# The last norm of a decoder layer: its first mean over five blocks of rows, not six

## The chip, the cores and the metric

The kernel runs on one core of a Trainium2 chip. The metric is the time of one execution on the device in microseconds (us), less is better. Before the change the median of three runs is 2515.79 us (2514.77 to 2517.98). All engines named are those of that core: TensorE (PE in the profile, with PEld for its weight loads), VectorE (DVE), ScalarE (ACT), GpSimd (POOL) and SyncE (SP), whose queue issues nearly all DMAs.

## What is computed

One decoder layer on eight sequences of 100 tokens, 1024 features each, in float32: a retention layer, a cross-attention over 722 context rows and the own tokens, and a gated feed-forward layer. After each of the three the input is added and the sum is normalised over the features. The change lies in the last of the three norms:

```python
def _layernorm(x, axis=-1, eps=1e-05):
    m = jnp.mean(x, axis=axis, keepdims=True)
    v = jnp.var(x, axis=axis, keepdims=True)
    return (x - m) / jnp.sqrt(v + eps)
...
    gate = jnp.einsum('bsd,hd->bsh', x, w_gate)
    up = jnp.einsum('bsd,hd->bsh', x, w_up)
    gated = jax.nn.silu(gate) * up
    return jnp.einsum('bsh,dh->bsd', gated, w_down)
...
x = _layernorm(x + _L0_ffn_ref(x, L0_ffn_w_gate, L0_ffn_w_up, L0_ffn_w_down), axis=-1)
```

## The kernel before

**Layout.** Activations lie with their features on the 128 partitions and the tokens along the free dimension. The 1024 features are KT = 8 blocks of rows, 0 to 7, and the 800 tokens two halves of N = 400. So y, the sum that is to be normalised, is eight tiles of 128 x 400 for each half, and a mean over the features is a sum over the eight blocks and over the partitions. The second is made on TensorE: a matmul whose weights are a 128 x 128 matrix with the same number everywhere (onem holds 1/1024; onem7 holds 1/896) leaves the column sum in all partitions of a PSUM tile.

**Products.** For float32 accuracy every operand is split into a high and a low part, and each product is three matmuls (L86 to L88 in mm3). The function proj makes one block of rows for one half: 8 x 3 = 24 matmuls of 128 x 400 into one PSUM bank. PSUM has banks of three tags: a (3), s (4) and v (1); acc_tag takes a and s in turn for successive calls.

**The last stage** (L976 to L1003). The hidden features of the feed-forward layer are worked through in four quarters. The first three use a scheme with seven products in place of eight; the last quarter is done here, block by block: proj multiplies block m of the last quarter's weights by z3[half], and L994 adds it to y[:, m], which holds the input and the other three quarters already. The first half of the tokens goes first; it splits the weights and keeps all eight, and the second half uses them again. There add_up (L254) also sums the blocks into s1.

**The norm of the first half** (norm_root, then scaled): when all eight blocks are there, the mean by one matmul (L279), eight subtractions (L281), eight squares on ScalarE (L260) summed on VectorE (L265), the variance by one matmul (L283), its inverse root by Ln and Exp on ScalarE and a correction step on VectorE (inv_root, L113 to L120), and eight multiplications (L271), each followed by the DMA of its block to the output. This runs while TensorE makes the products of the second half.

**The norm of the second half** would stand at the end with nothing behind it, so it is begun before all blocks are there. norm_early takes the mean of the blocks so far by one matmul (L294) and subtracts it from them (L297). The blocks that come later have the same number subtracted when their product is added (L993, L994). Then norm_more adds each of them to two sums that stay open in PSUM: delta (L305), which gives the distance of the true mean from the one that was used, and var (L299 for the early blocks' squares together, L306 for those of each later one). norm_late then takes the square of delta on ScalarE (L312), subtracts delta from all blocks (L316), takes the square of delta from var (L313), makes the inverse root, and calls scaled. In exact arithmetic the result is the same whichever blocks come early; the number of early blocks is the argument first, and the factor f = 7 / first turns onem7's 1/896 into the mean over first blocks:

```python
f = (KT - 1) / first
for m in range(first):
    nc.vector.scalar_tensor_tensor(y[:, m], mean, -f, y[:, m], ALU.mult, ALU.add)
```

norm_early, norm_more and norm_late also serve out_proj, where seven blocks come early (the default of first).

**What sets the order.** Each engine runs its own list of instructions strictly in order and waits on counters of the others. The lists are made when the program is built: a scheduler simulates a time line and takes, for each engine, the ready instruction of the highest priority, so an instruction can stand at another place of its list than in the text. Thus in the second half's last products the one of block 7 (its weights lie in the tile f, its bank has the tag a) stands ahead of the one of block 6 (weights z, tag s). Once built the order is fixed: if an instruction isn't ready in fact, everything behind it on its engine waits.

In the built program the end looks like this. TensorE: products of blocks 4, 5 and 7, L294, product of block 6, two L305, L299, two L306. VectorE: additions for blocks 4 and 5 with the eight multiplications of the first half (L271) between them, six L297, two L993, one L265, L994 for block 7, L994 for block 6, four L265, eight L316, L313, two steps of the root, eight L271. ScalarE: eight squares, with L312 between the sixth and the seventh, and the three steps of the root. A float32 matmul with unsplit operands (L279, L283, L294, L299, L305, L306) is shown as two matmul records.

Of the kernel before, what the change touches and what calls it, by code (L numbers as in the profile page):

```python
# [20 lines left out]
KT = D // P  # L21
# [18 lines left out]
def decoder_layer(ctx, tc, xT, cT, w1, wo1, w2, wo2, wc, w3, wd, gw, qw, kw, trig, dec, mask, out):  # L40
    nc = tc.nc

    def sbuf(name, bufs, side=None):
        return tc.tile_pool(name=name, bufs=bufs, side=side, reuse_waits="tile")
# [51 lines left out]
    def acc_tag():  # L96
        turn[0] += 1
        return "as"[turn[0] % 2]

    def proj(w, z, n=N, tag="a"):  # L100
        acc = bank(tag)[:, :n]
        for k in range(KT):
            t = z[k // QT]
            mmw(acc, w, k, t[:, 0, k % QT, :n], t[:, 1, k % QT, :n], k == 0, k == KT - 1)
        return acc
# [146 lines left out]
    def add_up(s1, y, m):  # L252
        if m > 0:
            nc.vector.tensor_tensor(s1, y[:, 0] if m == 1 else s1, y[:, m], ALU.add)  # L254
# [14 lines left out]
    def scaled(y, r, dst, z=None):  # L269
        for m in range(KT):  # L270
            nc.vector.scalar_tensor_tensor(y[:, m], y[:, m], -0.5, r, ALU.mult, ALU.mult)  # L271
            if z is not None:
                split(z[m // QT][:, :, m % QT], y[:, m])
            nc.sync.dma_start(out=dst(m), in_=y[:, m])

    def norm_root(y, s1, p):
        n = y.shape[2]
        mean = bank("s")[:, :n]
        nc.tensor.matmul(mean, onem, s1, start=True, stop=True)  # L279
        for m in range(KT):  # L280
            nc.vector.tensor_tensor(y[:, m], y[:, m], mean, ALU.subtract)  # L281
        var = bank("v")[:, :n]
        nc.tensor.matmul(var, onem, squares(y, p, range(KT)), start=True, stop=True)  # L283
        vs = p.tile([P, n], F32, tag="vs", name="vs")
        nc.scalar.copy(vs, var)
        return inv_root(p, vs, eps_ln, n)
# [4 lines left out]
    def norm_early(y, s1, p, first=KT - 1):  # L291
        n = y.shape[2]
        mean = bank("s")[:, :n]
        nc.tensor.matmul(mean, onem7, s1, start=True, stop=True)  # L294
# [3 lines that stand above are left out]
        var, delta = bank("v")[:, :n], bank("s")[:, :n]  # L298
        nc.tensor.matmul(var, onem, squares(y, p, range(first)), start=True, stop=False, skip_group_check=True)  # L299
        return mean, var, f, delta, first  # L300

    def norm_more(y, early, p, m):

        _, var, _, delta, first = early
        nc.tensor.matmul(delta, onem, y[:, m], start=m == first, stop=m == KT - 1, skip_group_check=True)  # L305
        nc.tensor.matmul(var, onem, squares(y, p, [m]), start=False, stop=m == KT - 1, skip_group_check=True)  # L306

    def norm_late(y, early, p, dst, z=None):
        _, var, _, delta, _ = early
        n = y.shape[2]  # L310
        vs = p.tile([P, n], F32, tag="vs", name="vs")
        nc.scalar.activation(vs, delta, AF.Square)  # L312
        nc.vector.tensor_tensor(vs, var, vs, ALU.subtract)  # L313
        r = inv_root(p, vs, eps_ln, n)
        for m in range(KT):
            nc.vector.tensor_tensor(y[:, m], y[:, m], delta, ALU.subtract)  # L316
        scaled(y, r, dst, z)
# [9 lines left out]
    def load_raw(src):  # L327
        st = wp.tile([P, KT * P], F32, tag="wst", name="wst", bufs=3)
        if isinstance(src, list):
            for i, s in enumerate(src):  # L330
                nc.sync.dma_start(out=st[:, i * H:(i + 1) * H].rearrange("p (u c) -> p u c", u=QT), in_=s)
        else:
            nc.sync.dma_start(out=st, in_=src)
        return st

    def w_split(src, w=None):
        if w is None:
            w = wp.tile([P, 2, KT * P], FR, tag="w", name="w", bufs=4)
        split(w, src)
        return w  # L340
# [573 lines left out]
    def next_slot():  # L914
        slots.append(slots.pop(0))
        return slots[-1]()
# [23 lines left out]
    def down_w(q, m):  # L940


        w = wd[q * QT:(q + 1) * QT, m // QT].rearrange("u p c -> p u c")
        c = m % QT * 2 * P
        return [w[:, :, c + i * P:c + (i + 1) * P] for i in range(2)]
# [31 lines left out]
    with sbuf("ln3", 2, "right") as lnp:  # L977
        ws = []
        for half in range(2):
            y = rows(half)  # L980
            s1 = lnp.tile([P, N], F32, tag="s1", name="s1", bufs=2)
            early = None
            for m in range(KT):
                if half == 0:
                    w = None
                    if m >= QT:
                        w = next_slot().rearrange("p l k n -> p l (k n)")[:, :, :KT * P]
                    ws.append(w_split(load_raw(down_w(QT - 1, m)), w))
                elif m == KT - 2:
                    early = norm_early(y, s1, lnp, m)  # L990
                acc = proj(ws[m], z3[half], tag=acc_tag())
                if early:
                    nc.vector.scalar_tensor_tensor(y[:, m], early[0], -early[2], y[:, m], ALU.mult, ALU.add)  # L993
                nc.vector.tensor_tensor(y[:, m], y[:, m], acc, ALU.add)  # L994
                if early:
                    norm_more(y, early, lnp, m)
                else:
                    add_up(s1, y, m)
            dst = lambda m, half=half: out[:, m, half * N:(half + 1) * N]
            if half == 0:  # L1000
                scaled(y, norm_root(y, s1, lnp), dst)
            else:
                norm_late(y, early, lnp, dst)  # L1003
# [71 lines left out]
```

## Time and profile before

| | |
|---|---|
| median of three runs | 2515.79 us (2514.77 to 2517.98) |
| the profiled execution's own time | 2517.7 us |
| its span, first to last instruction | 2515.9 us |
| TensorE busy in the span | 2465.4 us (98%) |
| VectorE, ScalarE, GpSimd busy | 1992.2, 1343.5, 481.2 us |
| mean granted TensorE clock | 0.993 |
| TensorE busy from 2480 to 2500 us | 18.89 of 20.00 |
| TensorE busy from 2500 us to the end | 2.30 of 16.00 |
| VectorE busy in the same two stretches | 13.91 and 10.28 |

The profile is of one execution; its time is 1.8 us more than its span, and 1.9 us more than the median of the runs. The page also draws the span in 40 slices of 63 us, busy tenths in each; the last of them holds the end of the last stage:

```profile
PE   8999999999899999999999999999999999999997
PEld 8999999999899999999999999999999999998997
DVE  7678876568989798899999999866987777666656
ACT  6667676335767565556566566533544544432221
```

TensorE is at nine tenths or more almost everywhere, so an engine beside it costs time only where TensorE waits for it, and at the very end, after TensorE's last product. That end, some 15 us, is where the changed lines stand. In the rows of the timeline the first number is the start in us from the span's beginning, the second the duration; a row that stands for several instructions (x6) has their duration together, and what stands in brackets is how long the engine was idle before the row and which instruction ended the wait.

### The profile page before, as it was taken

What the parts mean: (1) busy time and instruction counts of PE and PEld (TensorE: products, weight loads), DVE (VectorE), ACT (ScalarE), POOL (GpSimd) and SP (SyncE); (2) the same over time, 40 slices, a digit from 0 to 9 for tenths busy, and PEclk for the clock granted to TensorE, in tenths of its full rate; (3) what the DMA queues carried; (4) which work ended last, traced back from release to release, by engine and by line L of the source; (5) the groups of instructions that cost most, each with busy time, mean ns of one, the idle gap of its engine ahead of it and who ended that gap; (6) DMA issues with size and microseconds to landing.
All of it is one profiled execution on the core that took longest, in us unless ns stands there. A gap on an engine that the chain in (4) does not pass through costs nothing.

```text
span 2515.9 us, 37158 instructions
## 1 busy us (share of the span) xinstructions
PE 2465.4 (98%) x14036; PEld 2442.0 (97%) x14036; DVE 1992.2 (79%) x3110; ACT 1343.5 (53%) x2264; POOL 481.2 (19%) x234
## 2 busy tenths in 40 slices
PE   8999999999899999999999999999999999999997
PEld 8999999999899999999999999999999999998997
DVE  7678876568989798899999999866987777666656
ACT  6667676335767565556566566533544544432221
POOL 0111111002645334433433433100000000000000
PEclk9999999999999999999999999999999999999999
DMA  7334445774444654554554554574455445388731
GB/s 240 110 110 127 136 144 187 239 266 148 144 152 133 207 175 142 178 166 151 169 176 144 166 192 135 189 273 152 145 181 192 159 160 167 127 302 311 250 102 53
DMA packets 224450, 433.96 MB, mean 172 GB/s; under 512 B 47338, under 2 KB 168042, under 8 KB 211854
## 3 DMA queue, kind: packets, MB, share of 16 engines
q1 hardware_dynamic: 223118, 427.39, 50.7%
q0 software_dynamic: 1152, 4.19, 1.1%
q8 instruction: 110, 1.80, 0.3%
q14 instruction: 70, 0.57, 0.1%
HBM read 322.18 MB, written 109.35 MB: 172 GB/s over the span
## 4 chain that ended last, share of the span: by engine, by line
PE 89%; DVE 6%; ACT 1%; DMA 1%; issue 1%; SPq 0%; DVEq 0%; ACTq 0%
PE a L88 18%; PE a L86 18%; PE a L87 18%; PE s L88 9%; PE s L87 9%; PE s L86 9%; PE v L88 2%; PE v L86 2%; PE v L87 2%; PE s L491 1%; PE s L688 1%; DVE r L120 1%; DVE r L119 1%; PE s L148 1%; DMA tp<-in_xT 1%
## 5 line engine op out<-in xcount | busy, mean ns | idle before, releaser
L86 PE MATMUL a<-big,w 128*128 128x400 f32 (+2 forms) x1808 | 611.4, 339 | 11.7 <-ACT big L67 7.4
L87 PE MATMUL a<-big,w 128*128 128x400 f32 (+2 forms) x1808 | 611.1, 338 | 0.0
L88 PE MATMUL a<-big,w 128*128 128x400 f32 (+2 forms) x1808 | 609.7, 338 | 0.0
L67 ACT CAST w<-wst 128x1024 fp32r<-128x1024 f32 (+1 forms) x231 | 239.2, 1038 | 389.4 <-PE s L88 130.7
L68 DVE TENSOR_TENSOR w<-wst,w 128x1024 fp32r<-128x1024 f32 (+1 forms) x231 | 281.0, 1218 | 117.0 <-ACT w L67 115.1
L86 PEld LDWEIGHTS a<-big,w 128*128 128x128 f32 x1808 | 341.3, 189 | 13.3 <-ACT big L67 7.7
L87 PEld LDWEIGHTS a<-big,w 128*128 128x128 f32 x1808 | 342.0, 189 | 1.3 <-DVE big L68 0.3
L88 PEld LDWEIGHTS a<-big,w 128*128 128x128 f32 x1808 | 342.0, 189 | 0.9 <-DVE w L68 0.2
L86 PE MATMUL s<-big,w 128*128 128x400 f32 x664 | 230.6, 347 | 0.1
L87 PE MATMUL s<-big,w 128*128 128x400 f32 x664 | 229.2, 345 | 0.0
L88 PE MATMUL s<-big,w 128*128 128x400 f32 x664 | 229.1, 346 | 0.0
L125 POOL PARTITION_ALL_REDUCE ss<-sq x56 | 161.1, 2881 | 336.3 <-DMA zd<-y 167.0
L605 POOL PARTITION_ALL_REDUCE kss<-ksq x64 | 173.2, 2706 | 116.4 <-ACT ksq L604 115.7
L86 PE MATMUL a<-z,w 128*128 128x400 f32 x488 | 168.6, 346 | 8.0 <-ACT r L118 4.3
L88 PE MATMUL a<-z,w 128*128 128x400 f32 x488 | 169.4, 348 | 0.7 <-DVE w L68 0.7
L87 PE MATMUL a<-z,w 128*128 128x400 f32 x488 | 169.4, 347 | 0.0
L87 PE MATMUL s<-z,w 128*128 128x400 f32 x400 | 139.1, 348 | 2.4 <-DVE z L68 2.4
L86 PE MATMUL s<-z,w 128*128 128x400 f32 x400 | 139.9, 350 | 0.0
L88 PE MATMUL s<-z,w 128*128 128x400 f32 x400 | 139.4, 348 | 0.0
L722 ACT ACTIVATE s<-s,rk 128x400 f32<-128x400 f32 x160 | 87.7, 591 | 91.9 <-DVE sm L742 65.5
L86 PEld LDWEIGHTS s<-big,w 128*128 128x128 f32 x664 | 124.6, 188 | 1.4 <-ACT w L67 0.4
L87 PEld LDWEIGHTS s<-big,w 128*128 128x128 f32 x664 | 124.6, 188 | 1.1
(330 smaller groups left out, 5650.9 us busy)
## 6 DMA issues: line engine op xcount, KB each, us to landing
wst<-in_w SPq DMA_DIRECT2D x135, 512.0 KB
w<-wcd SPq DMA_DIRECT2D x64, 1024.0 KB
wst<-in_wo SPq DMA_DIRECT2D x64, 512.0 KB
hd<-h SPq DMA_DIRECT2D x12, 1400.0 KB
wst<-in_wd SPq DMA_DIRECT2D x64, 256.0 KB
big<-o1d SPq DMA_DIRECT2D x16, 800.0 KB
qd<-d SPq DMA_DIRECT2D x32, 400.0 KB
q<-qd SPq DMA_DIRECT2D x32, 400.0 KB
```

Source lines behind the costliest of these rows:

```text
L67: nc.scalar.copy(hi, src)
L68: nc.vector.tensor_tensor(lo, src, f32(hi), ALU.subtract)
L86: nc.tensor.matmul(acc, lh, rh, start=start, stop=False, skip_group_check=chain)
L87: nc.tensor.matmul(acc, lh, rl, start=False, stop=False, skip_group_check=chain)
L88: nc.tensor.matmul(acc, ll, rh, start=False, stop=stop, skip_group_check=chain)
L119: nc.vector.scalar_tensor_tensor(q, ss, eps, q, ALU.add, ALU.mult)
L120: nc.vector.scalar_tensor_tensor(q, q, 3.0, r, ALU.subtract, ALU.mult)
L125: nc.gpsimd.partition_all_reduce(y, x, P, op)
L148: nc.tensor.transpose(tr[0:T, b * P:(b + 1) * P], vt[:, b * T:(b + 1) * T], ident)
L491: nc.tensor.matmul(bt(o)[:, b], vv[:, b * P:(b + 1) * P], pf[:, b], start=True, stop=True)
L605: nc.gpsimd.partition_all_reduce(ss[:, at], sq[:, at], P, RED.add)
L722: nc.scalar.activation(sc, sp, AF.Copy, scale=rk[:, c:c + 1])
```

## The change

In the second half of the tokens, norm_early is called ahead of block 5 rather than block 6. It gets first = m, so five blocks (0 to 4) are summed, taken relative to their mean and squared early; blocks 5, 6 and 7 (before: 6 and 7) go through L993 and norm_more.

```diff
@@ -986,7 +986,7 @@
                     if m >= QT:
                         w = next_slot().rearrange("p l k n -> p l (k n)")[:, :, :KT * P]
                     ws.append(w_split(load_raw(down_w(QT - 1, m)), w))
-                elif m == KT - 2:
+                elif m == KT - 3:
                     early = norm_early(y, s1, lnp, m)
                 acc = proj(ws[m], z3[half], tag=acc_tag())
                 if early:
```

In the order of the built program this moves instructions on three engines. TensorE: L294 stands seven matmuls behind the start of block 7's product; where it stood, between the products of blocks 7 and 6, stands L305 for block 5; after the product of block 6 come L299, L306 for block 5, two L305 (blocks 6 and 7) and two L306. VectorE: behind the eight L271 of the first half come five L297, three L993, one L265, L994 for blocks 5 and 7, three L265, L994 for block 6, and then L316 as before. ScalarE: L312 stands behind all eight squares. The lists of GpSimd and SyncE are the same.

## The prediction

> **What bounds the kernel now.** The page's chain of waits says that TensorE bounds the whole, so I looked for the stretch in which another engine takes over, then read the timeline of that stretch.
>
> ```profile
> PE 89%; DVE 6%; ACT 1%; DMA 1%; issue 1%; SPq 0%; DVEq 0%; ACTq 0%
> ```
>
> Timeline (start, duration in us, engine, line, out<-in, idle before and its releaser), end of the program:
>
> ```profile
> 2484.52 0.57 DVE L254 TENSOR_TENSOR s<-s,y 128x400 f32<-128x400 f32 x1
> ...
> 2488.89 0.57 DVE L994 TENSOR_TENSOR y<-y,a 128x400 f32<-128x400 f32 x1
> 2488.99 0.35 PE L87 MATMUL a<-big,f 128*128 128x400 f32 x1
> ...
> 2491.91 0.34 PE L88 MATMUL a<-big,f 128*128 128x400 f32 x1
> 2492.09 0.83 PE L294 MATMUL s<-s,onem 128*128 128x400 f32 x2
> ...
> 2492.94 0.34 PE L87 MATMUL s<-big,z 128*128 128x400 f32 x1
> 2492.96 2.98 DVE L297 SCALAR_TENSOR_TENSOR y<-s,y 128x400 f32<-128x400 f32 x6 [2.90 <-PE s L294]
> ...
> 2495.86 1.04 DVE L993 SCALAR_TENSOR_TENSOR y<-s,y 128x400 f32<-128x400 f32 x2
> 2496.82 0.56 DVE L265 TENSOR_TENSOR s<-sq 128x400 f32<-128x400 f32 x1
> 2496.95 0.34 PE L88 MATMUL s<-big,z 128*128 128x400 f32 x1
> 2497.31 0.56 DVE L994 TENSOR_TENSOR y<-y,a 128x400 f32<-128x400 f32 x1
> 2497.79 0.56 DVE L994 TENSOR_TENSOR y<-y,s 128x400 f32<-128x400 f32 x1
> 2498.40 1.61 PE L305 MATMUL s<-y,onem 128*128 128x400 f32 x4 [1.10 <-DVE y L994]
> 2500.05 0.50 ACT L312 ACTIVATE vs<-s 128x400 f32<-128x400 f32 x1
> 2500.79 3.93 DVE L316 TENSOR_TENSOR y<-y,s 128x400 f32<-128x400 f32 x8
> ```
>
> TensorE feeds everything until the mean (L294), which stands between the product of block 7 (weights f, issued first) and that of block 6 (weights z). From 2492.96 on VectorE is almost never idle: its list behind the mean, not block 6's product, sets the end. The new mean could use VectorE's gap before 2492.96.
>
> **The change, part by part.** I read the order and the wait counts of both built programs; they differ only here. VectorE loses one L254 and one L265 and does five L297 and three L993 for six and two. ScalarE squares eight blocks either way. TensorE gets one L305 and one L306 more. No DMA is added or moved; SyncE's and GpSimd's queues are as they were.
>
> *The mean earlier.* L294 now stands behind seven matmuls of block 7's product, at 2488.99. It needs the sum over blocks 0 to 4, ready at 2484.52 + 0.57 = 2485.09, so it doesn't wait. VectorE starts L297 0.87 later (2492.09 to 2492.96 now): 2489.86. It has then finished the eight multiplies of the first half, whose next instruction starts at 2488.89 now.
>
> *VectorE until block 5 is complete.* Eight subtractions of the mean at 0.483 (2.90 / 6), 3.86, to 2493.72; one L265, 0.49 (2496.82 to 2497.31): block 5's L994 starts at 2494.21. This addition is now behind the subtractions; before, it ran at 2488.89, ahead of them.
>
> *The wait that the change adds.* L305 for block 5 stands on TensorE between the products of blocks 7 and 6, and waits for exactly that L994. A matmul starts 0.61 after such an addition starts (2497.79 to 2498.40): 2494.82. TensorE has issued the last of block 7 at 2491.91 + 0.67 (one such small product costs 2492.94 - 2492.09 less a normal step of 0.18) = 2492.58; with 0.34 that ends at 2492.92. So TensorE stands idle for 1.90 us. Queued behind L305 are block 6's 24 matmuls, and behind those the addition of block 6 and all that follows. L305 takes the place that L294 had, so block 6 starts 2494.82 - 2492.09 = 2.73 later; its last matmul at 2499.68, its L994 0.39 later (a row pair at 2483.16 and 2483.55) at 2500.07, so its L305 may start at 2500.68.
>
> *The tail.* TensorE first issues L299 and block 5's L306, ready long before, at 0.67 each from 2499.86 to 2501.20; then L305 for blocks 6 and 7 at 2501.20 and 2501.87. The step from the last L305 to L316 is shown bare in the other late norm:
>
> ```profile
> 1740.99 0.83 PE L305 MATMUL s<-y,onem 128*128 128x400 f32 x2
> ...
> 1741.86 0.50 ACT L312 ACTIVATE vs<-s 128x400 f32<-128x400 f32 x1 [2.77 <-PE s L305]
> 1742.39 3.94 DVE L316 TENSOR_TENSOR y<-y,s 128x400 f32<-128x400 f32 x8 [0.90 <-ACT vs L312]
> ```
>
> That is 0.87 + 0.53, so L316 starts at 2503.27 for 2500.79: **+2.5 us**. All behind it is unchanged: the last two L306 end at 2504.1, before L313 at 2507.1 asks for the variance. The two VectorE instructions saved (2 x 0.48) are worth nothing, as VectorE now waits for TensorE; if that wait is gone they come back.
>
> *What an idle TensorE does to its clock.* The trace shows no such stall at this place, so I bound it by all others. Windows (length, PE busy, ..., PEclk third from the end):
>
> ```profile
> 847.42:850.84 3.42, 1.52 (x11) 1.23 (x10) 1.31 (x5) 2.34 (x6) 0.00 (x0) 1.00 0.95 244
> 850.84:854.25 3.41, 3.41 (x14) 3.41 (x13) 1.98 (x8) 0.97 (x5) 0.00 (x0) 0.50 0.97 341
> ...
> 509.50:512.91 3.41, 2.04 (x11) 1.59 (x10) 1.90 (x3) 1.04 (x1) 0.00 (x0) 1.00 1.02 424
> 512.91:516.32 3.41, 3.41 (x20) 3.27 (x19) 3.41 (x8) 1.02 (x2) 0.00 (x0) 1.00 1.01 415
> ```
>
> The granted clock falls to a half at 608.49, 635.80, 676.76, 714.30, 850.84 and 2318.57, all whole multiples of 3.413 apart: it is decided on a fixed grid. I computed TensorE's busy time in every cell of it. Start-up aside, a full-clock cell with 1.52 busy or less is followed by one at half clock; one with 2.04 or more never is; none lies between. At half clock matmuls start 0.333 apart (2322.24 to 2322.57), not 0.182, so a cell loses 3.41 x (1 - 0.182 / 0.333) = 1.55 us, and all of it would fall into block 6's product. The cost is thus 0 or 1.55. A stall of 1.90 leaves 1.51 busy in a cell that holds all of it. With the limit at 1.52, 1.51 of 3.41 positions of the grid do that, 44%; with the limit at 2.04 (1.37 idle suffices, so 0.53 more on each side), 75%; halfway 60%. I take 1.55, by that majority.
>
> The Trainium skill says otherwise: "TensorE: Matmul & The Clock Gate", in its part on the HAM clock gate and that on HAM oscillation, lets the clock fall only after a whole idle window of about 3.4 us. By it this stall would cost nothing more and the sum would be +2.5; the row above, with 1.90 us idle and the next cell at 0.50, contradicts it.
>
> **Sum.** 2.5 + 1.55 = +4.0. The profiled execution has a span of 2515.9 and a time of 2517.7, 1.8 around it; it would become 2519.9 and 2521.7. It was 1.9 above the median of the runs; on that median, 2515.79 + 4.0 = 2519.8. That is 0.16%; a measurement of this kernel can tell about 0.2% (5.0 us) from no change, so I forecast a small loss that counts as no change.
>
> **Rivals.**
>
> *The stall without the clock.* As above, with the grid lying so that no cell sees too little work: 2515.79 + 2.5 = 2518.3. For it: 40% of positions by the halfway limit. Against it: the other 60%.
>
> *Clearly slower: two half-clock cells in a row.* At 2318.57 the first slow cell had 2.52 busy, and the next was slow too; at 676.75 one with 3.17 busy was not. So if a grid edge falls inside the stall, with at least 1.37 idle before it and at least 0.24 behind it, the clock stays low twice: 2.5 + 3.1 = 5.6, 2521.4, +0.22%. It decides from an edge between 2494.29 and 2494.58, 0.29 of 3.41 positions at the most, and with the strict limits (1.90 and 0.89) never.
>
> *Not slower: TensorE doesn't wait.* If block 5's addition is in time, block 6 starts only one small product (0.67) later; its last matmul at 2497.62, then L299, L306 and two L305 at 0.67, L316 at 2501.21: +0.4, 2516.2. For that VectorE would have to be 2 us quicker between the mean and L994 than its rows say. If moreover only VectorE's load counted, the two instructions saved would give -1.0, 2514.8. Against both: the rows of the nine instructions in front.
>
> That the change doesn't act is out: both orders show the mean moved.
>
> **How the numbers follow.** Stall and one slow cell 0.45; stall alone 0.38; two slow cells 0.05; no stall 0.12. Predicted: 2519.8. The range goes from 2516.2, the upper end of the no-stall case, to 2521.4, the two-cell case; within it lie all cases but part of the last and the scatter of the runs (2514.77 to 2517.98). Likeliest case alone: 2518.8 to 2520.8. Slower by over 0.2%: the two-cell case, and a fifth of the forecast, which lies 1.0 below the bound, with scatter: 0.05 + 0.09 = 0.14. Faster by over 0.2% would need -5.0, more than any term here; 0.01 for scatter. Within: 0.85.
>
> **What would show it.** Right: the mean near 2489, L297 five times from about 2489.9, an idle time of about 1.9 before L305 released by L994, block 6's product starting 2.7 later, VectorE idle before L994 of block 6 and before L316. The clock: 0.50 in one cell of 3.41 within block 6's product, and matmuls 0.333 apart. Wrong: L305 for block 5 without idle time; L316 starting before 2502; a difference before 2484, where both programs are equal; or a stall well above 1.9, which would make the slow cell certain.

## The result and the profile after

| | before | changed |
|---|---|---|
| median (lowest to highest) of 22 runs each | 2516.70 us (2514.77 to 2525.07) | 2520.84 us (2518.46 to 2527.34) |
| ratio, 95% interval | | 1.0015 [1.0008, 1.0022] |
| span of the profiled execution | 2515.9 | 2520.4 |
| from the first matmul of block 5's product to L316 | 17.44 | 21.59 |

The medians differ by 4.1 us, 0.16%; the forecast was +4.0. The interval of the ratio is 2.0 to 5.5 us, so the whole times leave room for the rival of +2.5 as well; it takes the traces to decide. In the text below, the distance from the first matmul of block 5's product to the first L316 is called the tail. It leaves out what varies from execution to execution ahead of the last stage, so it compares single traces to some hundredths of a us, where a few whole runs leave 2 us open. Its two ends before are the first matmul below and L316 at 2500.79; VectorE's row below stands directly ahead of that L316.

```profile
2483.35 0.34 PE L86 MATMUL a<-big 128*128 128x400 f32 x1
...
2498.27 2.60 DVE L265 TENSOR_TENSOR s<-s,sq 128x400 f32<-128x400 f32 x4
```

The timeline of the changed kernel, VectorE's rows first (columns as before):

```profile
2490.17 2.50 DVE L297 SCALAR_TENSOR_TENSOR y<-s,y 128x400 f32<-128x400 f32 x5 [0.88 <-PE s L294]
2492.59 1.53 DVE L993 SCALAR_TENSOR_TENSOR y<-s,y 128x400 f32<-128x400 f32 x3
2494.03 0.57 DVE L265 TENSOR_TENSOR s<-sq 128x400 f32<-128x400 f32 x1
2494.51 1.05 DVE L994 TENSOR_TENSOR y<-y,a 128x400 f32<-128x400 f32 x2
...
2502.03 0.57 DVE L994 TENSOR_TENSOR y<-y,s 128x400 f32<-128x400 f32 x1 [4.62 <-PE s L88]
2505.25 3.94 DVE L316 TENSOR_TENSOR y<-y,s 128x400 f32<-128x400 f32 x8 [2.65 <-ACT vs L312]
```

TensorE, from the start of the tail:

```profile
2483.66 0.34 PE L86 MATMUL a<-big 128*128 128x400 f32 x1
...
2489.30 0.83 PE L294 MATMUL s<-s,onem 128*128 128x400 f32 x2
...
2495.13 0.94 PE L305 MATMUL s<-y,onem 128*128 128x400 f32 x2 [1.90 <-DVE y L994]
...
2496.09 0.35 PE L87 MATMUL s<-big,z 128*128 128x400 f32 x1
...
2496.67 0.54 PE L87 MATMUL s<-big,z 128*128 128x400 f32 x1
2497.01 0.54 PE L88 MATMUL s<-big,z 128*128 128x400 f32 x1
...
2501.65 0.34 PE L88 MATMUL s<-big,z 128*128 128x400 f32 x1
2501.83 0.83 PE L299 MATMUL v<-s,onem 128*128 128x400 f32 x2
2502.50 0.83 PE L306 MATMUL v<-sq,onem 128*128 128x400 f32 x2
2503.18 1.51 PE L305 MATMUL s<-y,onem 128*128 128x400 f32 x4
```

The reader is to see two things. Before, VectorE waited 2.90 us for the mean and then ran without a gap; now it waits 0.88, but 4.62 for block 6's product and 2.65 for L312. The engine that sets the end has changed: the wait has gone from VectorE to TensorE, which stands idle for 1.90 us ahead of L305, released by block 5's addition. And from 2496.67 on the matmuls of block 6's product start 0.33 apart rather than 0.18. The windows of the cells around it (a cell is one step of the grid of 3.413 us on which the clock is set) show the granted clock at that place (PE busy first, then the other engines, the granted clock third from the end):

```profile
2493.15:2496.57 3.42, 1.52 (x7) 1.15 (x7) 3.32 (x8) 1.45 (x3) 0.00 (x0) 1.00 0.01 2
2496.57:2499.98 3.41, 3.41 (x12) 3.38 (x11) 0.73 (x2) 0.58 (x2) 0.00 (x0) 0.50 0.00 0
2499.98:2503.39 3.41, 3.41 (x16) 2.80 (x16) 0.57 (x1) 0.55 (x2) 0.00 (x0) 1.00 0.00 0
```

One cell with 1.52 us of work, then exactly one cell at half clock.

### The profile page after: what moved, and what is told of

The parts are those of the page before. It is cut to its first block, busy times and chain, and to the rows that moved or that the text cites. A ratio compares the mean times of both kernels' runs of the same rounds, so it can differ in the third digit from the quotient of the medians.

```text
span 2520.4 us, 37163 instructions
## 1 busy us (share of the span) xinstructions
PE 2469.7 (98%) x14040; PEld 2445.2 (97%) x14040; DVE 1993.9 (79%) x3108; ACT 1343.4 (53%) x2264; POOL 478.7 (19%) x234
## 4 chain that ended last, share of the span: by engine, by line
PE 89%; DVE 6%; DMA 2%; issue 1%; ACT 1%; SPq 0%; DVEq 0%; ACTq 0%
PE a L88 18%; PE a L86 18%; PE a L87 17%; PE s L88 10%; PE s L87 10%; PE s L86 9%; PE v L88 2%; PE v L86 2%; PE v L87 2%; PE s L491 1%; PE s L688 1%; DVE r L120 1%; DVE r L119 1%; PE s L148 1%; DVE d L68 1%
```

## The experiments

The theory: the loss is the wait of TensorE for block 5's addition, with 1.90 us of idle time ahead of L305 and L316 2.5 us later, and the half-clock cell that this idle time brings about, 1.55 us. The main rival: it is the added work, two small matmuls more and a longer row of statistics. Kernels are compared by the tail, where not said otherwise; the ratios are those to the kernel before on the same chip.

### The same work, block 5 first on VectorE (e3_first5)

The edit moves no instruction on TensorE; VectorE takes block 5's L993 and addition as soon as the mean is there, ahead of the five L297. (In this kernel the two steps of block 5 are shown as an L297 and L990.)

```diff
-        for m in range(first):
-            nc.vector.scalar_tensor_tensor(y[:, m], mean, -f, y[:, m], ALU.mult, ALU.add)
+        for m in ([first] if block else []) + list(range(first)):
+            i = nc.vector.scalar_tensor_tensor(y[:, m], mean, -f, y[:, m], ALU.mult, ALU.add); block and (block(y, m) if m == first else m == 0 and tc.keep_in_program_order(i))
...
-                    early = norm_early(y, s1, lnp, m)
+                    early = norm_early(y, s1, lnp, m, lambda y, m: nc.vector.tensor_tensor(y[:, m], y[:, m], proj(ws[m], z3[1], tag=acc_tag()), ALU.add))
...
```

> The same instructions as the changed kernel on every engine, TensorE in the same order; only VectorE takes the two steps of block 5 (L993, its addition) ahead of the five subtractions of the mean. Theory (stall): L305 of block 5 finds its input ready, no idle time before it, no half-clock cell, block 6's product 0.67 us later than before the change, L316 0.4 us later: +0.4 us, ratio 1.0002. Rival (work): nothing is removed, so +4 us as before, ratio 1.0015.

Measured: ratio 0.9999 [0.999, 1.0008]; tail 17.88, +0.44. The timeline, VectorE and TensorE:

```profile
2488.51 0.57 DVE L297 SCALAR_TENSOR_TENSOR y<-s,y 128x400 f32<-128x400 f32 x1 [0.88 <-PE s L294]
2489.12 0.57 DVE L990 TENSOR_TENSOR y<-y,a 128x400 f32<-128x400 f32 x1
2489.61 2.49 DVE L297 SCALAR_TENSOR_TENSOR y<-s,y 128x400 f32<-128x400 f32 x5
...
2499.88 3.94 DVE L316 TENSOR_TENSOR y<-y,s 128x400 f32<-128x400 f32 x8 [2.65 <-ACT vs L312]
```

```profile
2491.23 0.34 PE L88 MATMUL a<-big,f 128*128 128x400 f32 x1
2491.41 0.83 PE L305 MATMUL s<-y,onem 128*128 128x400 f32 x2
2491.78 0.65 PE L86 MATMUL s<-big,z 128*128 128x400 f32 x1
```

Block 5 is complete at 2489.69, well ahead of 2491.41, and L305's row has no idle time. The work is all still there and 3.7 of the 4.15 us are gone. The rival that blames the work for the whole loss falls; 0.44 us are left, which this kernel doesn't take apart.

### The idle time filled (e2_fill)

Two small matmuls are added ahead of L305 of block 5. They write to delta's bank, which L305 then overwrites; block 6's product is held behind L305 (d5 is that L305).

```diff
...
     def norm_more(y, early, p, m):
-
+        for i in range(2 * (early[4] == m == 5)): nc.tensor.matmul(early[3], onem, y[:, 4], start=True, stop=False, skip_group_check=True)
...
-                acc = proj(ws[m], z3[half], tag=acc_tag())
+                with tc.issue_after(d5.ins) if early and m == 6 else nullcontext(): acc = proj(ws[m], z3[half], tag=acc_tag())
```

> The changed kernel with two more small matmuls, whose result is overwritten, between block 7's product and L305 of block 5. Theory (stall and clock apart): L305 still starts when block 5's addition is done, at the same time; the idle time before it falls from 1.90 to about 0.57 us, no grid cell is under 2.8 us of work there, so the clock stays at 1.00 through block 6's product: +2.5 us over the kernel before in every execution, ratio 1.0010, although TensorE does 1.33 us more. If the clock had no part in it: +4 as in the changed kernel. Rival (work): 1.33 more than the changed kernel, +5.4 us, ratio 1.0021.

Measured: ratio 1.0014 [1.0005, 1.0023]; tail 20.06, +2.62. The idle time in the timeline, and the cells' windows:

```profile
2489.54 1.50 PE L303 MATMUL s<-y,onem 128*128 128x400 f32 x4
...
2491.60 0.94 PE L305 MATMUL s<-y,onem 128*128 128x400 f32 x2 [0.56 <-DVE y L994]
```

```profile
2488.17:2491.59 3.42, 2.88 (x13) 1.94 (x11) 3.42 (x9) 0.59 (x3) 0.00 (x0) 1.00 0.00 0
2491.59:2495.00 3.41, 3.40 (x17) 3.10 (x18) 2.08 (x4) 1.55 (x4) 0.00 (x0) 1.00 0.01 2
```

TensorE does two small matmuls more than in the changed kernel, some 1.3 us (the idle time falls from 1.90 to 0.56), L305 starts as late as there (11.47 us behind the first matmul of block 5's product), and the tail is 1.53 us shorter. That is the price of the half-clock cell, with the wait itself left in. The whole runs can't tell the two kernels apart; the trace does.

### The changed kernel again, and four single executions (a2_same, a3_look to a6_look)

> The changed kernel once more, beside the others on the same chip. Theory (stall): TensorE stands idle for 1.9 us before L305 of block 5, released by L994, in this execution too; block 6's product starts 2.7 us later than before the change. Whether the half-clock cell follows depends on where the grid lies: time over the kernel before +2.5 us without it, +4.0 with it, so a ratio between 1.0010 and 1.0016. Rival (work): the loss is the two more small matmuls and the longer statistics at the end; then the same +4, but with no part of it before block 6's product.

Measured: ratio 1.0014 [1.0005, 1.0023]; idle time 1.90, a half-clock cell, tail 21.59. So far every trace of the changed kernel had the slow cell, and the grid's part was not shown. Four more executions were traced for that; all four have the same expectation.

> The changed kernel once more, for its trace alone. Theory: the idle time before L305 of block 5 is 1.90 us each time, but the grid of 3.41 us lies at another place in each execution. If a grid cell holds at least 1.8 us of the idle time, the next one runs at half clock and L316 starts 21.6 us after the first matmul of block 5's product; if a grid edge cuts the idle time so that neither cell holds as much, the clock stays at 1.00 and the distance is 20.0 to 20.1. About half of the looks should be of each kind. Rival (any idle time of this length costs the clock, wherever the grid lies): 21.6 in all looks.

Measured: the idle time is 1.90 in all four; the tails are 21.59, 20.04, 21.63 and 20.04. Windows of the cells in the first (a3_look) and in the second (a4_look):

```profile
2488.64:2492.05 3.41, 1.51 (x7) 1.07 (x7) 3.31 (x8) 1.38 (x3) 0.00 (x0) 1.00 0.01 2
2492.05:2495.46 3.41, 3.41 (x12) 3.39 (x11) 0.81 (x2) 0.67 (x2) 0.00 (x0) 0.50 0.00 0
```

```profile
2488.53:2491.95 3.42, 1.76 (x10) 1.42 (x8) 3.42 (x8) 0.59 (x2) 0.00 (x0) 1.00 0.00 0
2491.95:2495.36 3.41, 3.17 (x16) 2.88 (x17) 2.30 (x5) 1.77 (x4) 0.00 (x0) 1.00 0.01 2
```

The same stall, cut by a grid edge in the second (its L305 starts at 2492.19, the edge is at 2491.95): 1.76 us of work in the cell, and no slow cell; in a6_look 1.82, and none. The rival that any stall of this length costs the clock falls. Six traces of the changed kernel: four with, two without. The whole times of the four (2517.76, 2517.70, 2521.26, 2516.95) don't show it: block 5's product starts at 2479.22, 2480.72, 2482.69 and 2479.97, so they differ by more than the price of a cell before the last stage begins. Start-up aside, five, five, six and five half-clock cells lie ahead of it, so their number alone doesn't explain the differences; the rest stays open.

### L305 of block 5 behind the products (e1_late)

```diff
+        d = nc.tensor.matmul(delta, onem, y[:, m], start=m == first, stop=m == KT - 1, skip_group_check=True); m == 5 and tc.keep_in_program_order(d)
...
+                for k in (range(5, m + 1) if early and m == 6 else [m] if early and m == 7 else []):
+                    norm_more(y, early, lnp, k)
```

> L305 of block 5 is pinned behind block 6's product; the scheduler then also puts most of block 7's product behind that of block 6, and two L305 (blocks 5 and 6) directly behind both. Theory (stall): no idle time between the products, both end as before the change; behind them two L305, L299, L306, L305 of block 7 at 0.67 each, L316 0.4 us later than before the change: +0.4 us, ratio 1.0002. Rival (work): as the changed kernel, +4 us, ratio 1.0015.

Measured: ratio 1.0002 [0.9993, 1.0011]; tail 17.87, +0.43; no idle time between the products. A second way of removing the wait gives the same as the first. VectorE again waits for L312:

```profile
2500.05 3.94 DVE L316 TENSOR_TENSOR y<-y,s 128x400 f32<-128x400 f32 x8 [3.32 <-ACT vs L312]
```

### The variance last (e4_delta_first), and one matmul less (e8_sum)

If the wait is all that spoils the change, the early mean should be of use once it is gone. Both kernels keep e1_late's order; the first puts all matmuls of the variance behind the last L305, the second also adds blocks 5 and 6 on VectorE before one L305 reads the sum (early[5] is the sum of the early blocks' squares).

```diff
+        for k in (range(first - 1, KT) if m == KT - 1 and len(early) > 5 else [] if len(early) > 5 else [m]): tc.keep_in_program_order(nc.tensor.matmul(var, onem, early[5] if k < first else squares(y, p, [k]), start=k < first, stop=k == KT - 1, skip_group_check=True))
...
+        if m == 6: t = p.tile([P, N], F32, tag="d56", name="d56", bufs=1); nc.vector.tensor_tensor(t, y[:, 5], y[:, 6], ALU.add)
+        if m != 5: tc.keep_in_program_order(nc.tensor.matmul(delta, onem, t if m == 6 else y[:, m], start=m == max(first, 6), stop=m == KT - 1, skip_group_check=True))
```

> As the kernel with block 5's L305 behind the products, and the four matmuls of the variance (L299 and three L306 before, now all on L306's line) behind the last L305. Theory (stall): with no idle TensorE between the products, what is left in front of L316 is the addition of block 7, the last L305 and L312. Three L305 stand directly behind the products at 0.67 each, the third reads block 7: L316 starts 0.9 us earlier than before the change, the variance is ready 1 us before L313 asks for it. -0.9 us, ratio 0.9996, beyond what the rounds can tell, so the trace decides: from the first matmul of block 5's product to L316 16.5 us, where the kernel before has 17.4 and the changed one 21.6. Rival (work): not below the kernel before.

Measured: ratio 1.0 [0.9991, 1.0009], by which it is told apart from neither kernel; tail 16.53, -0.91. VectorE:

```profile
2494.14 0.57 DVE L994 TENSOR_TENSOR y<-y,a 128x400 f32<-128x400 f32 x1 [0.23 <-PE a L88]
2496.70 3.94 DVE L316 TENSOR_TENSOR y<-y,s 128x400 f32<-128x400 f32 x8 [1.98 <-ACT vs L312]
```

> As the kernel with the variance behind, and blocks 5 and 6 added to each other on VectorE before one L305 reads them, so two L305 in place of three. Theory (stall): VectorE is idle while block 7's product runs, so the addition costs nothing; the last L305 starts as soon as block 7 is added, 0.5 us earlier: L316 1.4 us earlier than before the change, 16.0 us from the first matmul of block 5's product; ratio 0.9994. Rival (work): not below the kernel before.

Measured: ratio 0.9995 [0.9986, 1.0004]; tail 16.11, -1.33. TensorE behind the last matmul of the products:

```profile
2496.56 0.34 PE L88 MATMUL a<-big,f 128*128 128x400 f32 x1
2496.74 0.83 PE L305 MATMUL s<-d,onem 128*128 128x400 f32 x2
2497.57 0.94 PE L305 MATMUL s<-y,onem 128*128 128x400 f32 x2
2498.34 0.83 PE L306 MATMUL v<-s,onem 128*128 128x400 f32 x2
```

The first L305 fills the time in which block 7 is added, and only one more stands ahead of L312. By the whole runs, this kernel is faster than the changed one (the intervals of the two ratios don't meet) and not told apart from the kernel before; by the trace its tail is 1.33 us shorter than that of the kernel before.

### Four and seven early blocks (e5_four, e6_seven)

The edit is the number alone: KT - 4 or KT - 1 in place of KT - 3.

> Four early blocks, not five. The scheduler takes block 5's product ahead of block 4's, the mean ahead of block 4's, the first half's eight multiplies between the subtractions of the mean. Theory (stall): VectorE completes block 4 at nearly the time when TensorE reaches its L305, which then stands between the products of blocks 7 and 6: an idle time of 0.3 us, no half-clock cell. Two L305 more inside, L299 and two L306 in front of the last two L305: L316 2.2 us later than before the change, ratio 1.0009. Rival (fewer early blocks cost more by themselves): over the changed kernel's +4.

Measured: ratio 1.0015 [1.0006, 1.0024]. Block 5's product comes first here, so the distance is taken from the product behind that of block 3: 22.48 before (2478.31 to 2500.79), 24.87 here, +2.39. The idle time ahead of the first L305 is 0.33 and the clock stays:

```profile
2493.94 0.94 PE L305 MATMUL s<-y,onem 128*128 128x400 f32 x2 [0.33 <-DVE y L994]
```

The ratio holds the expected 1.0009 and doesn't tell it from the changed kernel's. So the kernel with four waits less than that with five and pays more for the statistics; fewer early blocks are not a scale on which the loss grows.

> Seven early blocks. The scheduler puts the mean behind all products, since the sum needs block 6. Theory: no stall between products, but all of VectorE's list (seven L297, L993, the sum of squares) then runs behind them, while TensorE is idle for about 5 us and loses its clock: L305 and the variance's matmuls run at half clock. L316 about 4 us later than before the change, and L313 then waits for the variance: +6 to +7 us, ratio 1.0026. Rival (the loss grows with the number of late blocks): below the kernel with six.

Measured: ratio 1.0027 [1.0018, 1.0037], the highest of all, though its interval overlaps those of the changed kernel and of four early blocks. L316 comes 4.10 us later than before, L313 6.84. TensorE and L313:

```profile
2501.26 1.70 PE L305 MATMUL s<-y,onem 128*128 128x400 f32 x2 [5.00 <-DVE y L994]
2507.37 1.70 PE L299 MATMUL v<-s,onem 128*128 128x400 f32 x2 [4.41 <-DVE s L265]
2508.86 1.54 PE L306 MATMUL v<-sq,onem 128*128 128x400 f32 x2
...
2510.44 0.57 DVE L313 TENSOR_TENSOR vs<-v,vs 128x400 f32<-128x400 f32 x1 [2.17 <-PE v L306]
```

The granted clock is 0.50 from 2498.35 on. A pair of small records takes 1.70 behind an idle time and 1.54 without one, where it takes 0.94 and 0.83 at full clock, and L313 waits 2.17 us for them.

## Why the prediction was right, point by point

- *The mean earlier.* Forecast: L294 behind seven matmuls, VectorE starts 0.87 later. Measured 0.87 (2489.30 to 2490.17).
- *VectorE until block 5.* Forecast: block 5's addition 4.35 us behind the first L297. Measured 4.34 (2490.17 to 2494.51).
- *The wait.* Forecast 1.90 us ahead of L305; measured 1.90 in each of the six traces. L305 starts 11.47 us behind the first matmul of block 5's product, as forecast. That both were exact comes from the order: every instruction between was of a kind that the trace of before already held, in the same shape.
- *Block 6's product.* Forecast 2.73 later; measured 2.84, from block 5's start to the second matmul of block 6's product (12.43 against 9.59). The 0.11 is the one term that was mis-sized: I took the price of L294, which ran in a full TensorE. Behind an idle time the pair takes 0.94 where it took 0.83. The trace of before had a row that shows it:

```profile
2500.93 0.94 PE L299 MATMUL v<-s,onem 128*128 128x400 f32 x2 [0.91 <-DVE s L265]
```

- *The tail.* Forecast: L316 2.5 us later, with L299 and block 5's L306 ahead of the last two L305. Measured 2.60 to 2.62 without the slow cell (a4_look, a6_look and e2_fill).
- *The clock.* Forecast: one half-clock cell, 1.55 us, by a majority of 60%. Measured 1.53 to 1.59 where it came (21.59 and 21.63 less 20.06 and 20.04), in four of six traces. The rival without it, +2.5, is what the other two executions showed; the forecast and its first rival are both true, each for a part of the executions, and a median over runs mixes them. That this median came within 0.1 us of the forecast difference is thus in part luck.
- *Two slow cells, no stall.* Neither occurred in the six traces. The third rival's reckoning for a kernel without the wait, +0.4, is what e3_first5 and e1_late gave when the wait was taken away.
- *VectorE's two saved instructions.* Forecast: worth nothing while VectorE waits for TensorE, and to be had if the wait goes. The second half is wrong. With the wait gone (e3_first5, e1_late), VectorE still stands idle for 2.65 and 3.32 us ahead of L316, and the tail is 0.44 longer. With the variance moved back too (e4_delta_first) the tail is 0.91 shorter, but VectorE still stands idle for 1.98 us there, more than the 0.96 of the two instructions, so the saving itself is not what sets the end. The rows speak for the earlier mean instead: before, two L994 and four L265 run without a gap between the last products and L316; in e4_delta_first only one L994 is left there. No run takes the one without the other.
- The absolute time, 2520.84 for a forecast 2519.8, is 1.0 higher, mostly because the median of before was itself 0.9 higher over 22 runs than over three. It lies just outside the 2518.8 to 2520.8 of the likeliest case alone.

## What to carry to other kernels

A sum that is made on the matmul engine stands in its queue like any other product, and if its input comes from a slower list on another engine, it holds up all that is queued behind it; so ask of each small matmul that is moved forward what is late at that place, and what stands behind it. Here the same early start lost 4 us; with two steps moved forward on the engine that feeds TensorE it lost 0.4, and with the small matmuls in another order it gained 1 in the trace. So finish the input of the next blocking step first, and put what nobody waits for last. When differences are below the scatter of whole runs, measure between two fixed instructions of the trace.

## What the runs showed of the hardware

The clock's grid was known from the trace of before; its rule came out sharper than I had it. Over all traces but that of e6_seven, start-up aside, a cell of 3.41 us at full clock was followed by a slow one when TensorE was busy for 1.52 us or less in it (with one exception, a cell at 1.52, in e1_late) and not when it was busy for 1.8 or more; between 1.6 and 1.8 there are cells of both kinds, and the cells' edges are known to about 0.05 us only. So a stall of 1.9 us was enough where it lay within a cell. The way back asks for more: in the profiled execution of the changed kernel a slow cell with 2.90 busy was followed by another slow one, and so was one with 3.00 in e3_first5, though one with 2.84 in a6_look was not. And the grid lies elsewhere in each execution, so the same kernel has several times; part of the scatter between the runs of the kernel before may come from this, which was not tested.
